# Opening of a two-layer attention kernel: weight sums on VectorE beside the first keys' product, bias columns and means in column tiles, vectors loaded as rows

## The chip, the core and the metric

The kernel runs on one core of a Trainium2 chip. The metric is the device time of one execution in microseconds (us); lower is better. The core has five engines with an instruction stream each: TensorE (PE, matrix products), VectorE (DVE), ScalarE (ACT), GpSimd (POOL) and SyncE (SP, which here only issues transfers). They wait for each other through semaphores. Transfers between the chip's memory (DRAM) and the on-chip memory (SBUF) run on 16 DMA engines. Matrix products are written to a small memory of their own, PSUM, in banks of 128 partitions x 512 float32 values.

## The reference

The input is `x`, 8 images of 512 channels by 32 x 32 points, in float32. Two layers follow each other, here cut to what is computed:

```python
# layer 0, on tokens: S = 1024 tokens of C = 512 channels per image
xn = layer_norm(x_flat, gamma, beta)                      # over channels, eps 1e-5
q = xn @ Wq.T + bq;  k = xn @ Wk.T + bk;  v = xn @ Wv.T + bv    # 8 heads of 64
attn = softmax(q @ k.T / sqrt(64))                        # per head
out = (attn @ v) @ Wo.T + bo + x_flat

# layer 1, on channels: group norm over 32 groups, then one head over all 512 channels
h = group_norm(x, gamma, beta)
q = wq @ h + bq;  k = wk @ h + bk;  v = wv @ h + bv
attn = softmax(q.T @ k * 512 ** -0.5)
out = x + wp @ (attn applied to v) + bp
```

## The kernel before

Almost every large product is done by a scheme of seven half-size products in place of eight (a Strassen-like one): both operands are cut into 2 x 2 blocks, some sums of blocks are formed (`S1` to `S4` of the weights, `T1` to `T4` of the data), and seven steps (`STEPS`) of matmuls follow, with additions on VectorE that put the results together. Weights are used again for each of the 8 images. Their blocks and sums are therefore formed once in the opening, saved to DRAM, and loaded again in each later image.

Two weight products are formed once as well: `a`, from the second layer's query and key weights, and `m`, from its value and output weights, so that the second layer needs fewer projections. With them come three small vectors: `ua` (the query bias carried through the key weights), `bm` and `bo` (value biases carried through the output weights).

Each engine runs the instructions in the order in which this program writes them (`ORDERED`: TensorE, ScalarE, VectorE; GpSimd's order is left to a scheduler). `later` puts a small piece of work into a list, and `tick` takes pieces from it between the steps of a product.

```python
STEPS = [
    ("11", "11", "x", True),
    ("12", "21", "z", True),
    ("S2", "T2", "x", False),
    ("S1", "T1", "y", True),
    ("S3", "T3", "x", False),
    ("22", "T4", "z", True),
    ("S4", "22", "y", False),
]
SLOTS = ["11", "12", "22", "S1", "S2", "S3", "S4"]
    # ... (cut)
    vt = const.tile([P, len(VECS), NC], F32, tag="vecs", name="vecs")
    with nc.allow_non_contiguous_dma(reason="per-channel vectors, once"):
        for i, n in enumerate(VECS):
            nc.scalar.dma_start(out=vt[:, i, :], in_=vecs[n].rearrange("(c p) -> p c", p=P))
    # ... (cut)
    wq, wk = (load_chunks(n) for n in ("q1", "k1"))
    bq1_row = half_tile("bq1_row")
    nc.sync.dma_start(out=bq1_row, in_=vecs["bq1"].rearrange("(a c) -> a c", a=1).to_broadcast((P, C)))
    x_next = load_x(0)
    wv, wp = (load_chunks(n) for n in ("v1", "p1"))
    # ... (cut)
    def sums_of_blocks(engine, w):
        engine.tensor_add(w["S1"], w["21"], w["22"])
        engine.tensor_sub(w["S2"], w["S1"], w["11"])
        engine.tensor_sub(w["S3"], w["11"], w["21"])
        engine.tensor_sub(w["S4"], w["12"], w["S2"])
    # ... (cut)
    def complete(n, w):

        sums_of_blocks(nc.gpsimd, w)
        save_w(n, w)
        return w

    wk_now, wv_now = first_w("k"), first_w("v")
    wo = first_w("o")
    wq_now = first_w("q")
    # ... (cut)
    def product(dst, lhs, rhs, n, g):
        ps = wide_psum(f"psw_{n}_{g}")
        for k in range(2):
            for oc in range(NC):
                nc.tensor.matmul(ps[:, ts(k, C)], lhs[oc][:, ts(2 * g + k, P)], rhs[oc],
                                 start=(oc == 0), stop=(oc == NC - 1))
        for i in range(2):
            nc.scalar.copy(dst[f"{i + 1}{g + 1}"], ps.rearrange("p (a o) -> p a o", a=2)[:, :, ts(i, CB)])

    def columns(dst, lhs, rhs, n, plus):

        ps = bank(f"ps{n}")
        for o in range(NC):
            for c in range(NC):
                nc.tensor.matmul(ps[:, o : o + 1], lhs(c, o), rhs(c), start=(c == 0), stop=(c == NC - 1))
        nc.vector.tensor_add(dst, ps[:, :NC], vt[:, VECS.index(plus), :])
    # ... (cut)
    # class Product: one of the seven steps
        def step(self, n=1):
            for _ in range(n):
                i = self.done
                self.done += 1
                a, b, to, opens = STEPS[i]
                until(lambda: a in self.a and b in self.b)
                if opens and not hasattr(self, to):
                    setattr(self, to, self.banks(to))
                self.part(getattr(self, to), self.a[a], self.b[b], opens)
                tick(self.pieces)
                if i == 0:
                    self.u1 = self.copy((0, 0))
                elif i == 1:
                    self.out(0, 0, self.u1, self.z)
                elif i == 2:
                    self.u2 = self.copy((0, 1))
                elif i == 4:
                    u3 = self.copy((1, 1))
                    self.out(1, 1, u3, self.y)
                    self.u3 = u3
                elif i == 5:
                    if self.shift.twice:
                        self.u3 = self.copy((1, 0))
                    self.out(1, 0, self.u3, self.z)
                elif i == 6:
                    self.out(0, 1, self.u2, self.y)
                if i in (2, 4, 6):
                    self.finish()
    # ... (cut)
    # class LayerNorm (for image b)
        def over_channels(self, ps):
            for k in range(NH):
                nc.tensor.matmul(ps[:, ts(k, HB)], ones_c, self.total[:, ts(k, HB)], start=True, stop=True)
    # ... (cut)
        def mean(self):
            ps = wide_psum(f"mean_{self.b}")
            self.over_channels(ps)
            self.mu = big_tile(f"mu_{self.b}")
            nc.scalar.copy(self.mu, ps)
    # ... (cut)
        def variance(self):

            ps = bank(f"var_{self.b}")
            for k in range(NH):
                nc.tensor.matmul(ps[ts(k, D), :], ones_c[:, :D], self.total[:, ts(k, HB)], start=True, stop=True)
            self.ps = ps
    # ... (cut)
    with tc.manual_schedule(engines=ORDERED):
        nq = natural(wq, "q1")
        nk = natural(wk, "k1")
        ln = LayerNorm(0, x_next)
        pieces = ln.steps()

        def norm(n):
            for _ in range(n):
                next(pieces, None)

        norm(5)
        wa = weight_tiles("a_first")
        product(wa, nq, nk, "a", 0)
        norm(3 + 4 + 3)
        nv = natural(wv, "v1")
        product(wa, nq, nk, "a", 1)
        columns(bm, lambda c, oc: wp[c][:, ts(oc, P)], lambda c: vec("bv1", c), "bm", "bp1")
        norm(100)
        for k in range(NH):
            for j in range(2):
                for a in range(2):
                    ln.affine(j, k, a)
        hb = operands(ln.result())
        add_operands(hb)
        until(lambda: not side)
        complete("k", wk_now)
        complete("v", wv_now)
        complete("o", wo)
        wm = weight_tiles("m_first")
        product(wm, nv, wp, "m", 0)
        columns(bo, lambda c, oc: wo[f"{oc // 2 + 1}{c // 2 + 1}"][:, c % 2, ts(oc % 2, P)],
                lambda c: vec("bv0", c), "bo", "bo0")
        product(wm, nv, wp, "m", 1)
        complete("q", wq_now)
        complete("a", wa)
        complete("m", wm)
        for c in range(NC):
            t = half_tile(f"uat_{c}")
            nc.vector.scalar_tensor_tensor(t, wk[c], 1.0, bq1_row, ALU.mult, ALU.mult, accum_out=ua[:, c : c + 1])
        kt = all_of(project("k0", wk_now, bias_of("bk0"), hb))
```

The sums that `complete` asks for, four for each of six sets of weights, run on GpSimd; `ua` is made by four VectorE instructions that multiply a 128 x 512 half of the key weights with the bias row and add up along the row. `columns` forms a vector by matmuls with one column each. A float32 matmul appears in the profile as two passes, so 16 matmuls are 32 records.

Of the kernel before, what the change touches and what calls it, by code (L numbers as in the profile page):

```python
# [11 lines left out]
F32 = mybir.dt.float32  # L12
# [4 lines left out]
ORDERED = {mybir.EngineType.PE, mybir.EngineType.Activation, mybir.EngineType.DVE}  # L17
# [48 lines left out]
def fast_path(ctx: ExitStack, tc: tile.TileContext, x: bass.AP, vecs: dict, weights: dict, out: bass.AP,  # L66
# [56 lines left out]

    def load_x(b):
# [33 lines left out]
    ident = const.tile([P, P], F32, tag="ident", name="ident")  # L158
    make_identity(nc, ident)
    ones_c = const.tile([P, P], F32, tag="ones_c", name="ones_c")  # L160
    nc.vector.memset(ones_c, 1.0 / C)
    ones = const.tile([P, P], F32, tag="ones", name="ones")
    nc.vector.memset(ones, 1.0)
    grp = const.tile([P, P], F32, tag="grp", name="grp")
    group_matrix(nc, grp)
    eps = const.tile([P, 1], F32, tag="eps", name="eps")
    nc.vector.memset(eps, EPS)
    checks = const.tile([P, B * (HEADS // 2 + 1)], F32, tag="checks", name="checks")
    nc.vector.memset(checks, 0.0)
    n_checks = [0]  # L170
# [70 lines left out]
    def complete(n, w):  # L241

        sums_of_blocks(nc.gpsimd, w)
        save_w(n, w)
        return w
# [3 lines left out]
    wq_now = first_w("q")  # L249

# [1149 lines left out]
```

## Time and profile before

| what | value |
|---|---|
| time, median of 3 runs | 3009.26 us (3009.22 to 3010.62) |
| span of the profiled execution | 3008.7 us |
| TensorE busy | 2965.4 us, 99% |
| VectorE busy | 1787.4 us, 59% |
| ScalarE busy | 1035.2 us, 34% |
| GpSimd busy | 47.9 us, 2% |
| moved by DMA | 217.34 MB, mean 72 GB/s |

The page gives the busy time of each engine, and also the span in 40 equal slices of about 75 us, with the busy share of each slice in tenths (9 is 90% or more). Here the opening is the first slice and part of the second:

```
PE   7999999999999999999999999999999999999898
POOL 5100000000000000000000000000000000000000
DMA  8003141031400313003120123101231021301201
```

GpSimd works in the opening and nearly nowhere else. Busy time of an engine includes the time in which an instruction has begun and is held up, so a busy engine is not always one that advances. The chain of waits is followed back from the last instruction to whatever released it, and lists pieces in order of time: what stands in it is what the end of the span waited for. A group line gives the line of the kernel, the engine, the operation, the tile written and the tiles read, the shape, the count, then busy time and the mean of one instruction in ns, then the idle time of the engine before them and what ended it.

### The profile page before, as it was taken

How to read it: one execution, taken by the hardware profiler on the slowest of the kernel's cores; microseconds unless marked ns; L12 is line 12 of the kernel's file. 1: busy time of each engine (PE TensorE's matmuls, PEld its weight loads, DVE VectorE, ACT ScalarE, POOL GpSimd, SP SyncE). 2: the span in 40 equal slices, each digit the busy share in tenths (PEclk: the TensorE clock that was granted, in tenths of full speed). 3: DMA queues.
4: the chain of work that ended last, by engine and by line, in shares of the span. 5: the costliest groups of instructions: out<-in, count | busy, mean ns of one | idle time of the engine just before them, and what ended most of it. 6: DMA issues, size and time to landing. Idle time of an engine off the chain costs nothing.

```text
span 3008.7 us, 26701 instructions
## 1 busy us (share of the span) xinstructions
PE 2965.4 (99%) x10066; PEld 1385.9 (46%) x10066; DVE 1787.4 (59%) x2241; ACT 1035.2 (34%) x1623; POOL 47.9 (2%) x57
## 2 busy tenths in 40 slices
PE   7999999999999999999999999999999999999898
PEld 4533455334553445434554345533455334553344
DVE  6567546674466744666547665467555675436744
ACT  3263213623146221551215512164222632125220
POOL 5100000000000000000000000000000000000000
PEclk9999999999999999999999999999999999999999
DMA  8003141031400313003120123101231021301201
GB/s 283 36 25 108 49 133 41 12 137 40 135 32 25 133 39 122 25 25 133 58 104 25 57 102 108 53 25 60 98 115 46 25 97 61 98 35 46 84 1 57
DMA packets 91162, 217.34 MB, mean 72 GB/s; under 512 B 14992, under 2 KB 19088, under 8 KB 91024
## 3 DMA queue, kind: packets, MB, share of 16 engines
q1 hardware_dynamic: 81616, 204.51, 19.6%
q0 software_dynamic: 3072, 11.01, 0.9%
q8 instruction: 81, 1.33, 0.2%
q10 hardware_dynamic: 6336, 0.03, 0.1%
q14 instruction: 57, 0.47, 0.1%
HBM read 156.26 MB, written 59.24 MB: 72 GB/s over the span
## 4 chain that ended last, share of the span: by engine, by line
PE 93%; DVE 3%; DMA 2%; issue 1%; ACT 0%; SPq 0%; DVEq 0%; ACTq 0%
PE s L657 15%; PE acc L672 14%; PE x_o L403 5%; PE x_s L395 5%; PE y_s L395 4%; PE y_o L403 4%; PE z_o L403 4%; PE z_s L395 4%; PE x_q L378 3%; PE x_vm L387 3%; PE x_qa L378 3%; PE x_v L387 3%; PE x_k L378 3%; PE y_k L378 2%; PE y_q L378 2%; PE z_qa L378 2%
## 5 line engine op out<-in xcount | busy, mean ns | idle before, releaser
L660 ACT ACTIVATE p<-s 128x1024 f32<-128x1024 f32 x512 | 476.3, 1057 | 85.2 <-PE s L657 85.2
L666 DVE TENSOR_TENSOR sum<-sum,p 128x1024 f32<-128x1024 f32 x384 | 470.5, 1225 | 41.4 <-DVE sum L666 0.9
L672 PE MATMUL acc<-p,v 128*64 128x512 f32 x2048 | 453.6, 595 | 0.0
L657 PE MATMUL s<-q,k_again 64*128 64x512 f32 x1792 | 403.3, 600 | 0.3
L672 PEld LDWEIGHTS acc<-p,v 128*64 128x64 f32 x2048 | 141.3, 137 | 305.1 <-issue 293.0
L657 PEld LDWEIGHTS s<-q,k_again 64*128 64x128 f32 x1792 | 161.8, 186 | 240.5 <-ACT p L660 120.1
L664 DVE TENSOR_TENSOR sum<-p,p 128x1024 f32<-128x1024 f32 x64 | 78.4, 1225 | 201.6 <-ACT p L660 201.6
L395 PE MATMUL x_s<-S_qa,T_gn 128*128 128x512 f32 x256 | 120.3, 592 | 0.0
L403 PE MATMUL x_o<-T_p,S_vm 128*128 128x512 f32 x256 | 115.1, 593 | 0.0
L675 ACT COPY o<-acc 128x512 f32<-128x512 f32 x64 | 37.5, 586 | 217.4 <-PE acc L672 217.0
L757 ACT ACTIVATE p<-p 128x512 f32<-128x512 f32 x128 | 80.7, 630 | 73.1 <-DVE p L317 73.1
L317 DVE TENSOR_TENSOR p<-u(1, 1)_s,y_s 128x512 f32<-128x512 f32 x32 | 22.0, 688 | 132.3 <-ACT u(1, 1)_s L408 132.3
L425 ACT ACTIVATE u(0, 0)_k<-x_k,vecs 128x512 f32<-128x512 f32 x16 | 11.0, 687 | 232.0 <-PE x_k L378 232.0
L694 ACT COPY rr<-r 32x16 f32<-32x16 f32 x256 | 51.6, 202 | 102.5 <-DVE r L631 99.4
L470 DVE STREAM_TRANSPOSE rden<-rr 128x512 f32<-128x512 f32 (+1 forms) x72 | 55.3, 768 | 37.0 <-ACT rr L694 23.4
L403 PEld LDWEIGHTS x_o<-T_p,S_vm 128*128 128x128 f32 x256 | 48.7, 190 | 61.2 <-issue 61.2
L395 PEld LDWEIGHTS x_s<-S_qa,T_gn 128*128 128x128 f32 x256 | 48.7, 190 | 61.2 <-issue 60.9
L317 DVE TENSOR_TENSOR y<-u(1, 1)_o,y_o 128x512 f32<-128x512 f32 x16 | 11.0, 688 | 109.1 <-ACT u(1, 1)_o L408 109.1
L378 PE MATMUL x_out<-T_o,w_o 128*128 128x512 f32 x128 | 61.5, 604 | 3.2 <-DVE T_o L457 3.2
L387 PE MATMUL x_vm<-w_m,T_gn 128*128 128x256 f32 x256 | 60.5, 379 | 0.0
L395 PE MATMUL y_s<-S_qa,gn 128*128 128x512 f32 x128 | 60.2, 593 | 0.0
L395 PE MATMUL x_s<-qa,gn 128*128 128x512 f32 x128 | 60.2, 592 | 0.0
(330 smaller groups left out, 4441.8 us busy)
## 6 DMA issues: line engine op xcount, KB each, us to landing
x<-in_x_dram SPq DMA_DIRECT2D x32, 512.0 KB, 7.8
xr<-in_x_dram SPq DMA_DIRECT2D x64, 256.0 KB, 4.2
x_away<-x SPq DMA_DIRECT2D x32, 512.0 KB, 2.8
x1r<-x_away SPq DMA_DIRECT2D x64, 256.0 KB, 3.3
out_dram<-y SPq DMA_DIRECT2D x64, 256.0 KB, 2.1
k_away<-k SPq DMA_DIRECT2D x28, 512.0 KB, 2.6
k_again<-k_away SPq DMA_DIRECT2D x28, 512.0 KB, 4.5
w_o<-saved_o SPq DMA_DIRECT2D x24, 512.0 KB, 5.4
```

What stands on the lines that cost most here:

```text
L378: nc.tensor.matmul(dst, a[:, k, ts(r, P)], b[:, k, :], start=(opens and k == 0), stop=(k == 1), skip_group_check=True)
L387: nc.tensor.matmul(dst[:, ts(m, CB)], b[:, k, ts(2 * r + m, P)], a[:, k, :], start=(opens and m == 0 and k == 0), stop=(k == 1), skip_grou ...
L395: nc.tensor.matmul(dst, b[:, k, ts(r, P)], a[:, k, :], start=(opens and k == 0), stop=(k == 1), skip_group_check=True)
L403: nc.tensor.matmul(dst, a[:, m, ts(r, P)], b[m // 2][:, m % 2, :], start=(opens and m == 0), stop=(m == NM // 2 - 1), skip_group_check=True)
L470: nc.vector.transpose(t.rearrange("p (k i) -> p k i", i=BL), r.unsqueeze(2).to_broadcast((P, r.shape[1], BL)))
L657: nc.tensor.matmul(s[:, ts(i, HB)], self.k[m // 4][r, ts(m % 4, P)], self.q[r, :], start=True, stop=True)
L660: nc.scalar.activation(p, s, AF.Exp, scale=1.0 / float(D) ** 0.5)
L664: nc.vector.tensor_add(self.sum, self.p[0], p)
L666: nc.vector.tensor_add(self.sum, self.sum, p)
L672: nc.tensor.matmul(acc[i * D : (i + 1) * D, :], value_of(self.vt, m, self.c * P + i * D, D), self.p[m][:, ts(i, HB)], start=(m == 0), stop ...
L694: nc.scalar.copy(rr[n][ts(j, BL), :], r[ts(2 * n + j // 2, BL), :])
L757: nc.scalar.activation(dest(i, k), dest(i, k), AF.Exp, scale=float(C) ** -0.5)
```

## The change

The change is to the opening, and to the mean of each layer norm.

- The sums `S1` to `S4` of the first layer's key weights stay on GpSimd, and are asked for at the very start. Those of the five other sets (`v`, `q`, `o`, `a`, `m`), and the four instructions for `ua`, become pieces for VectorE, two of which are taken between any two steps of the first keys' product. GpSimd's order is now fixed by the program too, and it issues the saves. This is for keeping GpSimd's arithmetic from running beside VectorE's, and for letting the keys' product begin before the sums are all there.
- `bm` and `bo` are made differently: the bias vector is set into the first column of four 32-column tiles of zeros, each of which takes one 128-row part of the weights and writes to 32 partitions of its own in one bank; a ones column then adds up the four rows. This replaces many matmuls of one column by a few long ones in column tiles.
- The mean of a layer norm is written as two tiles of 64 columns, one for each half of the tokens, into one bank, as the variance was before. Four copies on ScalarE then spread it to all partitions, where one copy did before.
- The twelve vectors are loaded as 48 rows of 128 contiguous values, and turned into columns by one transpose on TensorE, instead of being scattered by the transfer value by value. The broadcast bias row for `ua` is loaded after the weights instead of before `x`.

The diff, without its parts that only move lines:

```diff
@@ -14,7 +14,8 @@
-ORDERED = {mybir.EngineType.PE, mybir.EngineType.Activation, mybir.EngineType.DVE}
+POOL = mybir.EngineType.Pool
+ORDERED = {mybir.EngineType.PE, mybir.EngineType.Activation, mybir.EngineType.DVE, POOL}
@@ constants (moved here from below the loads, cut) @@
+    with tc.manual_schedule(engines={POOL}):
... (cut: the same constants)
+    vrows = const.tile([len(VECS) * NC, P], F32, tag="vrows", name="vrows")
+    for i, n in enumerate(VECS):
+        nc.scalar.dma_start(out=vrows[ts(i, NC), :], in_=vecs[n].rearrange("(c p) -> c p", p=P))
+    vt = const.tile([P, len(VECS), NC], F32, tag="vecs", name="vecs")
@@ -129,11 +150,6 @@
-    vt = const.tile([P, len(VECS), NC], F32, tag="vecs", name="vecs")
-    with nc.allow_non_contiguous_dma(reason="per-channel vectors, once"):
-        for i, n in enumerate(VECS):
-            nc.scalar.dma_start(out=vt[:, i, :], in_=vecs[n].rearrange("(c p) -> p c", p=P))
-
     def vec(n, c):
         i = VECS.index(n)
         return vt[:, i, c : c + 1]
@@ loads (constants moved up, cut) @@
     wq, wk = (load_chunks(n) for n in ("q1", "k1"))
-    bq1_row = half_tile("bq1_row")
-    nc.sync.dma_start(out=bq1_row, in_=vecs["bq1"].rearrange("(a c) -> a c", a=1).to_broadcast((P, C)))
     x_next = load_x(0)
     wv, wp = (load_chunks(n) for n in ("v1", "p1"))
... (cut: constants moved up)
+    bq1_row = half_tile("bq1_row")
@@ -209,14 +209,16 @@
             d, t = saved_part(n, w, g)
             nc.gpsimd.dma_start(out=d, in_=t)
 
-    def sums_of_blocks(engine, w):
-        engine.tensor_add(w["S1"], w["21"], w["22"])
-        engine.tensor_sub(w["S2"], w["S1"], w["11"])
-        engine.tensor_sub(w["S3"], w["11"], w["21"])
-        engine.tensor_sub(w["S4"], w["12"], w["S2"])
-
     SUMS = {"S1": ("add", "21", "22"), "S2": ("subtract", "S1", "11"), "S3": ("subtract", "11", "21"),
             "S4": ("subtract", "12", "S2")}
+
+    def sum_of_blocks(engine, w, n):
+        op, l, r = SUMS[n]
+        engine.tensor_tensor(w[n], w[l], w[r], getattr(ALU, op))
+
+    def sums_of_blocks(engine, w):
+        for n in SLOTS[3:]:
+            sum_of_blocks(engine, w, n)
 
     def sum_later(w, n, new, view):
 
@@ -242,11 +244,17 @@
 
         sums_of_blocks(nc.gpsimd, w)
         save_w(n, w)
-        return w
+
+    def complete_later(n, w):
+
+        for name in SLOTS[3:]:
+            later(lambda name=name: sum_of_blocks(nc.vector, w, name))
+        later(lambda: save_w(n, w))
 
     wk_now, wv_now = first_w("k"), first_w("v")
     wo = first_w("o")
     wq_now = first_w("q")
+    nc.sync.dma_start(out=bq1_row, in_=vecs["bq1"].rearrange("(a c) -> a c", a=1).to_broadcast((P, C)))
 
     def natural(t, n):
 
@@ -271,13 +279,29 @@
         for i in range(2):
             nc.scalar.copy(dst[f"{i + 1}{g + 1}"], ps.rearrange("p (a o) -> p a o", a=2)[:, :, ts(i, CB)])
 
-    def columns(dst, lhs, rhs, n, plus):
-
-        ps = bank(f"ps{n}")
-        for o in range(NC):
+    class Columns:
+
+
+
+        def __init__(self, dst, v, plus):
+            self.dst, self.v, self.plus = dst, VECS.index(v), VECS.index(plus)
+            self.z = half_tile(f"z_{v}").rearrange("p (c i) -> p c i", i=BL)[:, :NC, :]
+            nc.vector.memset(self.z, 0.0)
+            nc.vector.tensor_copy(self.z[:, :, 0], vt[:, self.v, :])
+
+        def rows(self, w):
+            ps = bank("ps_rows")
             for c in range(NC):
-                nc.tensor.matmul(ps[:, o : o + 1], lhs(c, o), rhs(c), start=(c == 0), stop=(c == NC - 1))
-        nc.vector.tensor_add(dst, ps[:, :NC], vt[:, VECS.index(plus), :])
+                for cols, part in w(c):
+                    nc.tensor.matmul(ps[ts(c, BL), cols], self.z[:, c, :], part, start=True, stop=True)
+            self.r = half_tile("rows")
+            nc.scalar.copy(self.r, ps)
+
+        def columns(self):
+            ps = bank("ps_columns")
+            for o in range(NC):
+                nc.tensor.matmul(ps[:, o : o + 1], self.r[:, ts(o, P)], ones[:, :1], start=True, stop=True)
+            nc.vector.tensor_add(self.dst, ps[:, :NC], vt[:, self.plus, :])
 
 
 
@@ -488,8 +512,9 @@
             self.b, self.xt = b, xt
 
         def over_channels(self, ps):
+
             for k in range(NH):
-                nc.tensor.matmul(ps[:, ts(k, HB)], ones_c, self.total[:, ts(k, HB)], start=True, stop=True)
+                nc.tensor.matmul(ps[ts(k, D), :], ones_c[:, :D], self.total[:, ts(k, HB)], start=True, stop=True)
 
         def add(self, name, k, l, r):
 
@@ -502,10 +527,12 @@
             yield
 
         def mean(self):
-            ps = wide_psum(f"mean_{self.b}")
+            ps = bank(f"mean_{self.b}")
             self.over_channels(ps)
             self.mu = big_tile(f"mu_{self.b}")
-            nc.scalar.copy(self.mu, ps)
+            for k in range(NH):
+                for r in range(2):
+                    nc.scalar.copy(self.mu[ts(r, D), ts(k, HB)], ps[ts(k, D), :])
 
         def rows(self, t, k):
             return t[:, ts(k, HB)].unsqueeze(1).to_broadcast((P, 2, HB))
@@ -518,11 +545,8 @@
             nc.scalar.activation(wide(self.sq[j, k]), wide(self.xt[j, k]), AF.Square)
 
         def variance(self):
-
-            ps = bank(f"var_{self.b}")
-            for k in range(NH):
-                nc.tensor.matmul(ps[ts(k, D), :], ones_c[:, :D], self.total[:, ts(k, HB)], start=True, stop=True)
-            self.ps = ps
+            self.ps = bank(f"var_{self.b}")
+            self.over_channels(self.ps)
 
         def root(self):
             self.var = compact(half_tile(f"vart_{self.b}"), self.ps)
@@ -873,13 +892,19 @@
             for _ in range(n):
                 next(pieces, None)
 
+        complete("k", wk_now)
         norm(5)
         wa = weight_tiles("a_first")
         product(wa, nq, nk, "a", 0)
+        ps = bank("ps_vecs")
+        nc.tensor.transpose(ps[:, : len(VECS) * NC], vrows, ident[: len(VECS) * NC, : len(VECS) * NC])
+        nc.vector.tensor_copy(vt.rearrange("p v c -> p (v c)"), ps[:, : len(VECS) * NC])
+        bm_columns, bo_columns = Columns(bm, "bv1", "bp1"), Columns(bo, "bv0", "bo0")
         norm(3 + 4 + 3)
         nv = natural(wv, "v1")
+        bm_columns.rows(lambda c: [(slice(0, C), wp[c])])
         product(wa, nq, nk, "a", 1)
-        columns(bm, lambda c, oc: wp[c][:, ts(oc, P)], lambda c: vec("bv1", c), "bm", "bp1")
+        bm_columns.columns()
         norm(100)
         for k in range(NH):
             for j in range(2):
@@ -888,21 +913,24 @@
         hb = operands(ln.result())
         add_operands(hb)
         until(lambda: not side)
-        complete("k", wk_now)
-        complete("v", wv_now)
-        complete("o", wo)
         wm = weight_tiles("m_first")
         product(wm, nv, wp, "m", 0)
-        columns(bo, lambda c, oc: wo[f"{oc // 2 + 1}{c // 2 + 1}"][:, c % 2, ts(oc % 2, P)],
-                lambda c: vec("bv0", c), "bo", "bo0")
+        bo_columns.rows(lambda c: [(ts(i, CB), wo[f"{i + 1}{c // 2 + 1}"][:, c % 2, :]) for i in range(2)])
         product(wm, nv, wp, "m", 1)
-        complete("q", wq_now)
-        complete("a", wa)
-        complete("m", wm)
-        for c in range(NC):
+        bo_columns.columns()
+
+        def score_bias(c):
             t = half_tile(f"uat_{c}")
             nc.vector.scalar_tensor_tensor(t, wk[c], 1.0, bq1_row, ALU.mult, ALU.mult, accum_out=ua[:, c : c + 1])
-        kt = all_of(project("k0", wk_now, bias_of("bk0"), hb))
+
+        for n, w in (("v", wv_now), ("q", wq_now), ("o", wo), ("a", wa), ("m", wm)):
+            complete_later(n, w)
+        later(*(lambda c=c: score_bias(c) for c in range(NC)))
+        units, kt = project("k0", wk_now, bias_of("bk0"), hb)
+        for u in units:
+            u.pieces = 2
+            u.rest()
+        until(lambda: not side)
 
         def next_values_and_queries(b, wv, wq):
```

More of the change, by code (lines that the diff above doesn't have):

```diff
@@ L121, in fast_path @@
         name=nc.get_next_instruction_name(), act_func_set_id=list(tables).index("natural_log_exp_and_others")))
+    with tc.manual_schedule(engines={POOL}):
+        ident = const.tile([P, P], F32, tag="ident", name="ident")
+        make_identity(nc, ident)
+        ones_c = const.tile([P, P], F32, tag="ones_c", name="ones_c")
+        nc.vector.memset(ones_c, 1.0 / C)
+        ones = const.tile([P, P], F32, tag="ones", name="ones")
+        nc.vector.memset(ones, 1.0)
+        grp = const.tile([P, P], F32, tag="grp", name="grp")
+        group_matrix(nc, grp)
+        eps = const.tile([P, 1], F32, tag="eps", name="eps")
+        nc.vector.memset(eps, EPS)
+        checks = const.tile([P, B * (HEADS // 2 + 1)], F32, tag="checks", name="checks")
+        nc.vector.memset(checks, 0.0)
+        n_checks = [0]
+    vrows = const.tile([len(VECS) * NC, P], F32, tag="vrows", name="vrows")
+    for i, n in enumerate(VECS):
+        nc.scalar.dma_start(out=vrows[ts(i, NC), :], in_=vecs[n].rearrange("(c p) -> c p", p=P))
+    vt = const.tile([P, len(VECS), NC], F32, tag="vecs", name="vecs")
     def load_x(b):
@@ L151, in fast_path @@
     wq, wk = (load_chunks(n) for n in ("q1", "k1"))
-    bq1_row = half_tile("bq1_row")
-    nc.sync.dma_start(out=bq1_row, in_=vecs["bq1"].rearrange("(a c) -> a c", a=1).to_broadcast((P, C)))
     x_next = load_x(0)
     wv, wp = (load_chunks(n) for n in ("v1", "p1"))
[L158 to L170, printed above, removed]
+    bq1_row = half_tile("bq1_row")
     ua = const.tile([P, NC], F32, tag="ua", name="ua")
@@ L859, in bias_of @@
         return lambda oc: vec(n, oc)
-    def all_of(units):
-        for u in units[0]:
-            u.rest()
-        return units[1]
     with tc.manual_schedule(engines=ORDERED):
```

## The prediction

> **What bounds the kernel now.** I read the busy shares first, then the chain of waits for the first 200 us, then the timeline of that stretch engine by engine, because the page says TensorE is 99% busy over the span (2965.4 of 3008.7 us) and only the first of its 40 slices is below 9 tenths by much. TensorE is the bound; what can be won is either TensorE work or TensorE idleness, and the idleness lies in the opening. The chain there (start us, us, what):
>
> ```profile
> 57.11 4.41 DVE T_h L457
> 61.52 0.39 issue
> 61.92 0.15 DVE bo L280
> 62.06 18.47 DVE uat L904 x8
> 80.53 0.61 DVE k L317
> 81.14 0.04 issue
> 81.19 3.78 PE z_k L378 x4
> 84.97 2.73 PE y_k L378 x4
> 87.70 1.72 PE x_k L378 x4
> ```
>
> TensorE stands behind four VectorE products (`uat`, L904) for 14.6 us: they sit in VectorE's order ahead of the first addition that frees a bank of the keys' product. Then the same four matmul passes that take 1.72 us at full clock take 3.78 and 2.73: 3.1 us more. The stretches of 10 us show it (columns after the stretch: TensorE, weight loads, VectorE, ScalarE, GpSimd busy with instruction counts, clock, DMA share, GB/s):
>
> ```profile
> 60.00:70.00 10.00, 6.61 (x16) 2.66 (x14) 10.00 (x5) 2.42 (x4) 9.97 (x11) 0.99 0.40 157
> 70.00:80.00 10.00, 0.00 (x0) 0.00 (x0) 10.00 (x5) 0.00 (x0) 9.97 (x12) 0.50 0.41 158
> 80.00:90.00 10.00, 8.81 (x14) 3.86 (x15) 3.11 (x6) 0.55 (x1) 3.34 (x5) 0.66 0.48 185
> ```
>
> VectorE is "busy" with five instructions in 10 us, and GpSimd is full. The groups of the first 100 us say why:
>
> ```profile
> L904 DVE SCALAR_TENSOR_TENSOR uat<-w_k,bq_row 128x512 f32<-128x512 f32 x4 | 18.5, 4685 | 0.0
> L501 DVE TENSOR_TENSOR lns<-lns 128x512 f32<-128x512 f32 x2 | 1.4, 691 | 0.1
> L545 DVE TENSOR_TENSOR x<-x,rstd 128x1024 f32<-128x1024 f32 x4 | 7.3, 1880 | 0.0
> L514 DVE TENSOR_TENSOR x<-x,mu 128x1024 f32<-128x1024 f32 x4 | 4.6, 1221 | 2.3 <-ACT mu L508 2.3
> L524 PE MATMUL var<-lnq,ones_c 128*64 128x512 f32 x4 | 2.9, 1086 | 0.0
> ```
>
> A 128x512 operation on two SBUF operands costs 0.69 us when GpSimd rests (L501) and 4.69 us beside its sums. In the timeline each `uat` ends while GpSimd issues transfers between two groups of sums. The scaling of L545 (1.88 against 1.22 for the same shape in L514) and the four `T_h` (11.5 us together from 50.48 to 62.0, against 4 x 1.22 = 4.9) are stretched likewise.
>
> [...] 4.69 against 0.69 us, while the `k` additions at 80.46 and 81.06, one operand in PSUM, take 0.68 us beside a running GpSimd sum. [...] the eight passes of a `den` (four 32-column tiles) stand 1.0 us apart from what follows, the four passes of a later `var` (two 64-column tiles) take 1.01 us, and the four of a `mean` over all 128 columns 1.72 us. [...] The trace agrees at 70 to 80 us (0.50 after 14.6 us idle), and shows also 0.50 in 36 to 38 us, just after the 32 one-column `psbm` passes (the four `var` passes take 2.9 us there)[...]. [...] In the trace the vectors' queue moves 0.03 MB in 6336 packets, for 3.5% of the first 100 us, so 3.5 us of every DMA engine.
>
> **The change part by part.**
>
> 1. *Sums leave GpSimd.* Of six sets of four, one (`k`) stays there, and runs when its blocks land; 20 sums go to VectorE between the keys' steps, two pieces a step. Cost on VectorE: 20 x 0.69 = 13.8, the four `uat` now uncontended at about 0.77 (0.69 + 0.08 for the accumulator read, an estimate) = 3.1, the eight additions 8 x 0.69 = 5.5: 22.4 us. The keys' product is 14 steps x 1.72 = 24.1 us on TensorE. VectorE fits, with little room. Laying its order against the steps, the additions that TensorE waits for still end about when they are needed, and VectorE finishes its last pieces some 2 us after TensorE; the value product that follows loads VectorE to half (4.0 and 5.2 of 10 us at 100 to 120), so this is absorbed. Before, the stage took from 57.87 (first `x_k`) to 99.60 (first `x_v`): 41.7 us. After: 24.1 plus about 0.7 of small waits, 24.8. Gain 17 us, of which 14.6 is the stall and 3.1 the clock.
>
> 2. *The start of the keys' product.* First load side: the vector packets (3.5 us per DMA engine) and the 0.26 MB bias row ahead of `x` go away. The second half of `w_k` waits for the second half of `w_q` to land, in both kernels; with clear queues I put `w_q` whole at about 5.5, `w_k` at 8.5, ScalarE free of issues at about 7.5, its copies of about 1 us after that, and the first `psw_a` at 11 instead of 14.36. Then TensorE's own work to `x_k`: `psw_a` 7.1, transposed vectors 0.3, `mean` 1.0, `pst_v` 1.9, bias rows 1.1 (column tiles, as `den`), `psw_a` 7.1, columns (8 one-column passes x 0.11) 0.9, `var` 1.2, `psw_m` 7.1, rows 1.1, `psw_m` 7.1, columns 0.9: 36.8 us, so 48 if nothing is waited for. Before, these places held 2 x 3.6 us of one-column passes, and the slow clock after each (`var` 2.9 instead of 1.0; the second `psw_m` 8.8 instead of 7.1).
>    But `var` waits for VectorE: mean at 19, its copies from ScalarE now in four of 0.59 (two are enough to start), centring from 20.2: 4.9, squares' sums 3.8; and GpSimd's four `k` sums (4 x 1.3 = 5) now fall just there, as the blocks land at about 22. 20.2 + 8.7 + 5 = 33.9, where TensorE could begin `var` at 30 (11 + 7.1 + 0.3 + 1.0 + 1.9 + 1.1 + 7.1 + 0.9): a wait of 3.5 us, perhaps with a slow clock after it. From there TensorE needs 17.4 to `x_k` (51.3), VectorE 0.7 + 4.0 + 4.9 + 4.9 + small = 15 to the last `T_h` (49), now without GpSimd. So `x_k` at about 52 with a share for the clock, against 57.87. Gain 6 us.
>
> 3. *Means in column tiles, seven more times.* Passes 1.72 become 1.01, and the next group takes 1.91 instead of 1.72, as behind `var`: 0.52 each, 7 x 0.52 = 3.6 us. It is TensorE work in a row without gaps, so it counts. The copies grow on ScalarE from 1.01 to 4 x 0.59 = 2.3 us, in a stretch where it is a quarter busy; the next `u` copy then ends about 3.0 us after the mean, while TensorE needs it at 3.4.
>
> Sum: 17 + 6 + 3.6 = 26.6 us; 3009.3 - 26.6 = 2982.7. I say 2982.5.
>
> **The rivals.** (a) VectorE becomes the bound of the keys' stage: 22.4 us of 24.1, with two-SBUF operations everywhere. Against: no GpSimd arithmetic is left then, only issuing; at 75 to 80 us a `uat` ended during such issuing, so issuing doesn't hold VectorE off. If it did, or if the `uat` form costs more than 0.77, the stage takes 28 to 30: about 2987. (b) The 14.6 us stall was hidden anyway by a later wait. Against: from 99.6 on the chain is TensorE step after step, without a wait up to 200 us; nothing there gives time back. If half were lost, 2990. (c) The early `k` sums hold VectorE off more than once over, as they did `uat`, and the late saves (9 MB, five sets, now packed into some 25 us, near the 390 to 410 GB/s seen at 20 to 40 us) delay the tiles that wait for their buffers: the value product's third result waits for a save. I put that save's landing at 25 us after the product begins, and the need at some 33. If late by 5 us: 2988. (d) The loads gain more, the collision misses `var`, and `x_k` starts at 48: 2978.
>
> **Range and chances.** The 14.6 us stall is nearly sure to go, and the means' 3.6 are copied from a measured neighbour; 20 us are solid. The spread comes from the opening's start (plus or minus 4) and the tightness of VectorE (up to 5). 8 in 10: 2976 to 2990. Two per cent are 60 us, and the whole stage that is touched is 100 us of which TensorE needs over 60; faster by over 2% has 0.01. Slower by over 2% needs a new stall in every batch, and the order of instructions after the opening is the same but for the means: 0.01.
>
> **What would show it.** Right: no TensorE idleness above 2 us between the first `x_k` and `x_v`, 25 us apart; `uat` below 1 us; sums near 0.69; clock at full through 50 to 80 us; `mean` four passes in 1.0 us in every batch; first `psw_a` near 11. Wrong: sums well above 0.69 us beside GpSimd's issues; the `k` additions as what TensorE waits for; `var` later than 36; a wait for a save at the third value result; or waits on `mu` that TensorE feels in later batches.

## The result and the profile after

| | before | after |
|---|---|---|
| time, median of 4 runs, measured together | 3009.94 us (3009.22 to 3011.54) | 2983.94 us (2980.97 to 2986.1) |
| span of the profiled execution | 3008.7 us | 2983.8 us |
| TensorE busy | 2965.4 us | 2956.7 us |
| first `x_k` (start of the first keys' product) | 57.87 us | 53.43 us |
| first `x_v` (its end) | 99.60 us | 77.71 us |

The ratio is 0.9912 (95%: 0.9895 to 0.9929), 26 us less. The two last rows are starts in the timeline; the chain puts the same starts up to 0.2 us later.

The chain of waits of the changed kernel, in order of time (start us, us, what), from layer norm's sums of squares to the next layer norm's mean:

```profile
27.09 2.23 DVE lnq L522
...
29.34 1.65 DVE lnq L526
30.99 2.20 DVE lnq L522
33.19 0.07 DVE bm L304
33.27 1.61 DVE lnq L526
...
34.91 1.94 PE var L517 x2
36.85 7.84 PE psw_m L277 x16
44.70 1.02 PE ps_rows L296 x16
45.72 7.06 PE psw_m L277 x16
52.78 0.79 PE ps_columns L303 x8
53.57 1.83 PE x_k L402 x4
55.40 1.72 PE z_k L402 x4
...
76.11 1.77 PE y_k L402 x4
77.87 1.73 PE x_v L411 x8
...
93.41 1.01 PE mean L517 x4
94.42 1.92 PE x_v L411 x8
```

Where `uat` stood for 18.47 us and `z_k` then took 3.78, there are now 14 steps of 1.72 to 1.83 us in a row. What VectorE holds up in the opening now is the variance: four `lnq` operations end one behind the other before the second half of `var`. The bias rows and columns are 1.02 and 0.79 us long. The stretches of 10 us show the same stage (columns as in the table of before):

```profile
50.00:60.00 10.00, 10.00 (x31) 4.93 (x30) 6.87 (x12) 2.45 (x4) 2.66 (x5) 1.00 0.40 159
60.00:70.00 10.00, 10.00 (x25) 4.31 (x24) 7.35 (x13) 1.95 (x3) 4.60 (x9) 1.00 0.91 351
70.00:80.00 10.00, 10.00 (x30) 5.30 (x29) 7.46 (x17) 2.32 (x4) 2.85 (x6) 1.00 0.94 357
```

TensorE is full and at clock 1.00, and VectorE does 12 to 17 instructions in 10 us where it did five. GpSimd's busy time is the issue of saves only. The VectorE groups of the first 80 us (shape and count, then busy us and mean ns of one, then idle before):

```profile
L522 DVE TENSOR_TENSOR lnq<-sq,sq 128x1024 f32<-128x1024 f32 x2 | 4.6, 2290 | 0.0
L526 DVE TENSOR_TENSOR lnq<-lnq 128x512 f32<-128x512 f32 x2 | 3.3, 1642 | 0.0
L217 DVE TENSOR_TENSOR w_a_first<-w_a_first,w_a_first 128x512 f32<-128x512 f32 x4 | 2.7, 688 | 0.0
L924 DVE SCALAR_TENSOR_TENSOR uat<-w_k,bq_row 128x512 f32<-128x512 f32 x4 | 2.7, 686 | 0.0
L481 DVE TENSOR_TENSOR T_h<-x,T_h 128x1024 f32<-128x1024 f32 x2 | 2.4, 1224 | 0.2 <-ACT x L573 0.2
```

`uat` fell from 4685 to 686 ns and `T_h` is at 1224 ns, while `lnq` is at 2290 ns in the shape in which `T_h` takes 1224: it runs beside the only sums left on GpSimd. In the waits of TensorE (us in total, times, longest) the 14.6 us of `z_k` are gone and one for `var` is new; the one for `T_o`, in the last image, is as before:

```profile
PE x_out L402 <- DVE T_o L481: 3.2, 1, 3.2
PE var L517 <- DVE lnq L526: 1.5, 1, 1.5
```

### The profile page after: what moved, and what is told of

It reads as the page before. It is cut to its first block, busy times and chain, and to the rows that moved or that the text cites. A ratio compares the mean times of both kernels' runs of the same rounds, so it can differ in the third digit from the quotient of the medians.

```text
span 2983.8 us, 26676 instructions
## 1 busy us (share of the span) xinstructions
PE 2956.7 (99%) x10043; PEld 1374.4 (46%) x10043; DVE 1777.3 (60%) x2266; ACT 1047.1 (35%) x1649; POOL 22.0 (1%) x37
## 4 chain that ended last, share of the span: by engine, by line
PE 97%; DVE 2%; DMA 1%; issue 0%; ACT 0%; SPq 0%; DVEq 0%
PE s L681 15%; PE acc L696 15%; PE x_o L427 6%; PE x_s L419 6%; PE y_s L419 4%; PE y_o L427 4%; PE z_s L419 4%; PE z_o L427 4%; PE x_q L402 3%; PE x_k L402 3%; PE x_qa L402 3%; PE x_vm L411 3%; PE x_v L411 3%; PE x_out L402 2%; PE y_k L402 2%; PE y_q L402 2%
```

## The experiments

Two questions were open. Which of the four parts makes which share? And is it the move of the sums to VectorE that removes the stall, or only the new place of the four `uat`, which now stand behind additions for which they used to hold TensorE? Ten other kernels answer, and the changed kernel was timed once more beside two of them. All keep the whole computation. First the table, with starts from the timeline of each (us), stage = first `x_v` less first `x_k`, and the median time against the kernel before in the same comparison:

| kernel | first x_k | first x_v | stage | time | before | ratio (95%) |
|---|---|---|---|---|---|---|
| before | 57.87 | 99.60 | 41.7 | | | |
| changed | 53.43 | 77.71 | 24.3 | 2983.94 | 3009.94 | 0.9912 (0.9895 to 0.9929) |
| only the sums | 61.07 | 85.27 | 24.2 | 2995.64 | 3012.22 | 0.9945 (0.9928 to 0.9962) |
| only `uat` behind | 59.60 | 83.80 | 24.2 | 2994.58 | 3012.22 | 0.9941 (0.9924 to 0.9957) |
| only the means | 59.62 | 101.36 | 41.7 | 3007.93 | 3012.22 | 0.9987 (0.9980 to 0.9994) |
| only the columns | 52.96 | 94.64 | 41.7 | 3005.32 | 3012.22 | 0.9976 (0.9968 to 0.9985) |
| only the vectors | 56.16 | 96.14 | 40.0 | 3008.92 | 3012.18 | 0.9989 (0.9981 to 0.9998) |
| changed, no columns | 56.74 | 80.93 | 24.2 | 2986.20 | 3012.18 | 0.9914 (0.9898 to 0.9931) |
| changed, no rows | 56.17 | 80.45 | 24.3 | 2986.52 | 3012.18 | 0.9915 (0.9896 to 0.9934) |
| changed, GpSimd sums | 49.95 | 74.23 | 24.3 | 2979.50 | 3012.18 | 0.9890 (0.9874 to 0.9907) |
| changed, again | 52.89 | 77.17 | 24.3 | 2983.01 | 3011.90 | 0.9901 (0.9884 to 0.9917) |
| changed, `k` sums on VectorE | 50.18 | 74.40 | 24.2 | 2979.66 | 3011.90 | 0.9892 (0.9875 to 0.9908) |
| changed, `uat` ahead, GpSimd sums | 48.95 | 91.06 | 42.1 | 2994.47 | 3011.90 | 0.9942 (0.9925 to 0.9958) |

One kernel's times spread by 1.7 us (four runs) to 10.9 us (twenty), so where two kernels differ by 3 us the trace carries the reading and the time only agrees. Starts in a trace spread too: two profiles of the changed kernel differ by 0.5 us at the first `x_k`, and the kernel with only `uat` behind, whose instructions up to there are those of the kernel before, begins the product 1.7 us later, because the end of `x` landed later (VectorE's sum of it begins at 22.10 us instead of 20.50). Durations within a chain are the safer reading.

### Only the sums

The kernel before with the sums and `uat` as pieces between the keys' steps, GpSimd's order fixed, and the early `k` sums:

```diff
+        complete("k", wk_now)
         norm(5)
...
-        complete("k", wk_now)
-        complete("v", wv_now)
-        complete("o", wo)
...
-        complete("q", wq_now); complete("a", wa); complete("m", wm)
-        for c in range(NC): ...  # the four uat
-        kt = all_of(project("k0", wk_now, bias_of("bk0"), hb))
+        for n, w in (("v", wv_now), ("q", wq_now), ("o", wo), ("a", wa), ("m", wm)):
+            complete_later(n, w)
+        later(*(lambda c=c: score_bias(c) for c in range(NC)))
+        units, kt = project("k0", wk_now, bias_of("bk0"), hb)
+        for u in units: u.pieces = 2; u.rest()
```

> The kernel before with the first part of the change alone: key sums early on GpSimd, the other 20 sums and the four uat as VectorE pieces beside the keys' product; vectors, bias columns and means as before. My theory [...]: the keys' stage, first x_k to first x_v, falls from 41.7 to about 25 us; uat below 1 us; first x_k stays within 2 us of 57.9, since TensorE is dense up to it; time about 3009.9 - 16 = 2994. Rival (the stage is short in the changed kernel only because the other parts bring x and the weights earlier): the stage stays above 30 us, time above 3000.

Measured: 16.6 us less. The stage is 24.2 us, 17.5 shorter, so the rival, that the other parts make it short, is refuted. The product begins 3.2 us later than before, not within 2 us as expected. Of this, 1.7 us is the spread just named; against the kernel with only `uat` behind, where `x` landed as late, the rest is `psbm` at 4.43 us instead of 3.47 and the first `psw_m` at 8.01 instead of 7.50.

### Only `uat` behind the keys' product

Two statements of the kernel before change places; every sum stays on GpSimd:

```diff
         complete("m", wm)
+        kt = all_of(project("k0", wk_now, bias_of("bk0"), hb))
         for c in range(NC):
             t = half_tile(f"uat_{c}")
             nc.vector.scalar_tensor_tensor(t, wk[c], 1.0, bq1_row, ALU.mult, ALU.mult, accum_out=ua[:, c : c + 1])
-        kt = all_of(project("k0", wk_now, bias_of("bk0"), hb))
```

> The kernel before with one thing moved: the four uat stand behind the eight additions of the keys' product in VectorE's order; all sums stay on GpSimd. Theory A (it is the order: slow two-SBUF operations stand ahead of additions that don't collide): no stall although GpSimd sums go on beside the product, stage about 25 us, additions 0.69 us, T_h still stretched, time about 2993. Theory B (the sums have to leave GpSimd for the stage to run): additions stretched as uat was, or uat again holding up the value product, stage or what follows it still over 35 us, time above 3002.

Measured: 17.6 us less, as much as the sums' move brings. The timeline (start us, us, engine, line, operation, count, and in brackets the idle time before and its end) shows why the sums may stay:

```profile
74.97 1.27 POOL L216 TENSOR_TENSOR w_a_first<-w_a_first,w_a_first 128x512 f32<-128x512 f32 x1
...
75.44 0.69 DVE L317 TENSOR_TENSOR k<-u(0, 0)_k,z_k 128x512 f32<-128x512 f32 x1 [2.82 <-PE z_k L378]
...
84.61 0.68 DVE L905 SCALAR_TENSOR_TENSOR uat<-w_k,bq_row 128x512 f32<-128x512 f32 x1
```

The addition `k`, which frees the bank TensorE waits for, reads one operand from PSUM and takes 0.69 us in the midst of a GpSimd sum. All eight additions of the product took 0.69 us, and GpSimd's last sum ended at 82.82 us, before `uat` begins at 84.61. So the whole stall came through four VectorE instructions in front of a fifth that GpSimd did not hold up.

### Only the means

`over_channels` and `mean` as in the change, in all eight layer norms, nothing else.

> The kernel before with only the means in two 64-column tiles and four copies. My theory: 0.6 to 0.7 us of TensorE work less in each of seven later images, the first one hidden in the opening, nothing else moves: about 3009.9 - 4.5 = 3005.4. Rival (the longer copies on ScalarE delay a copy that TensorE waits for): period from mean to mean not below 363.9 us, time 3009 or more.

Measured: 4.3 us less by 20 runs, as expected (the 95% interval of the ratio means 1.8 to 6.0 us). The start of the first product says nothing here: its own profiled execution was a long one for this kernel (span 3010.7 us).

### Only the columns

`Columns` in place of `columns`, in the kernel before:

```diff
-    def columns(dst, lhs, rhs, n, plus):
...
-                nc.tensor.matmul(ps[:, o : o + 1], lhs(c, o), rhs(c), start=(c == 0), stop=(c == NC - 1))
+    class Columns:
...
+                    nc.tensor.matmul(ps[ts(c, BL), cols], self.z[:, c, :], part, start=True, stop=True)
```

> The kernel before with only the bias columns made through rows in 32-column tiles. TensorE saves 2 x 2 us and the slow clock behind each group (1.9 and 1.7 us), so x_k may start 4 to 7 us earlier. Theory A (that start is hidden behind the uat stall, whose end is set by VectorE and GpSimd): stall longer by as much, time within 2 us of before. Theory B (it counts by itself): 3003 to 3005.

Measured: 6.9 us less (3005.32). The theory that the stall would swallow this gain fell. The chain:

```profile
34.45 0.79 PE ps_columns L295 x8
35.24 1.94 PE var L540 x4
...
47.94 2.79 DVE T_h L473
50.83 5.87 DVE T_h L473 x3
...
57.43 18.50 DVE uat L922 x8
76.58 3.78 PE z_k L394 x4
...
94.80 1.73 PE x_v L403 x8
```

The stall is untouched (`uat` 18.50 us, stage 41.7), but it begins 4.6 us sooner, at 57.43 instead of 62.06. The bias passes stood ahead of `var`, and behind `var` come the scaling and the `T_h`, and behind these `uat`. A stall swallows a gain only if its end is set from elsewhere; this one is a piece of VectorE work, 18.5 us long, whose start hung on the same TensorE work. But that path carries only 1.0 of the 4.6 us. VectorE's timeline has the scaling and the last `T_h`, first in the kernel before, then here:

```profile
43.28 7.28 DVE L545 TENSOR_TENSOR x<-x,rstd 128x1024 f32<-128x1024 f32 x4
57.11 4.88 DVE L457 TENSOR_TENSOR T_h<-x,T_h 128x1024 f32<-128x1024 f32 x1
...
42.30 5.71 DVE L561 TENSOR_TENSOR x<-x,rstd 128x1024 f32<-128x1024 f32 x4
55.07 2.29 DVE L473 TENSOR_TENSOR T_h<-x,T_h 128x1024 f32<-128x1024 f32 x1
```

The scaling begins 1.0 us sooner; it then takes 1.6 us less and the last `T_h` 2.6 less beside GpSimd's sums, the first three `T_h` 0.5 more. So most of the gain is two-input VectorE work that met GpSimd's sums at other moments. No run shows whether that would hold with other loads.

### Only the vectors

Rows and one transposition, and the bias row for `uat` after the weights:

```diff
-            nc.scalar.dma_start(out=vt[:, i, :], in_=vecs[n].rearrange("(c p) -> p c", p=P))
+    for i, n in enumerate(VECS):
+        nc.scalar.dma_start(out=vrows[ts(i, NC), :], in_=vecs[n].rearrange("(c p) -> c p", p=P))
...
+        nc.tensor.transpose(ps[:, : len(VECS) * NC], vrows, ident[: len(VECS) * NC, : len(VECS) * NC])
```

> The kernel before with only the vectors loaded as rows (one transpose to columns) and the bias row loaded after the weights. Before on the chip of the earlier runs was 3012.2. Theory A (loads land earlier, so the layer norm and with it the uat stall start and end earlier): first psw_a near 12.2 us instead of 14.4, x at 18 instead of 20.5 or later, stall unchanged in length, time 2 to 3 us below before. Theory B (hidden, as the stall's end hangs on GpSimd's sums): within 1 us of before.

Measured: 3.3 us less (3008.92; the 95% interval of the ratio means 0.6 to 5.7 us), first `x_v` 3.5 us sooner. The first `psw_a` begins at 12.20 instead of 14.36 us, and the first `x_k` 1.7 us sooner; the rest is in the stage, where TensorE waits 13.3 us instead of 14.6.

### The changed kernel with the old columns

> The changed kernel with the bias columns made as before by one-column matmuls. Bias columns alone gave 6.9 us in the kernel before. Theory A (they lie on TensorE's and the layer norm's path here too): x_k 5 to 7 us later than 53.6, slow clock again behind both groups, time 5 to 7 us above the changed kernel's 2984. Theory B (here the wait for var covers the first group): 3 to 4 us above.

The edit takes `Columns` out of the changed kernel and puts `columns` back. Measured: 2986.20 us, 2.3 and 3.2 us above the two medians of the changed kernel, and in the trace 3.2 us later at the first `x_v`; the theory of 5 to 7 us was wrong, the rival's 3 to 4 about right. The chain shows what the columns removed:

```profile
29.51 4.58 PE psbm L287 x32
34.09 2.82 PE var L501 x4
36.92 7.85 PE psw_m L277 x16
44.76 3.47 PE psbo L287 x32
48.23 8.67 PE psw_m L277 x16
```

`psbm` here lies within the time in which the changed kernel waits for `lnq`, so removing it saved nothing: `var` ends at 36.91 us here and at 36.85 there, and the `psw_m` behind it takes 7.85 and 7.84. The second vector counts whole: `psbo` and the `psw_m` after it, 3.47 + 8.67 = 12.1, against 1.02 + 7.06 + 0.79 = 8.9 in the changed kernel, 3.3 us.

### The changed kernel with the vectors loaded value by value

> The changed kernel with the vectors loaded value by value as before (12 transfers of 512 elements; the bias row stays late). Theory A (the start of the loads is on the path): psw_a at 14 instead of 12.2, x_k 1.5 to 3 us later, time 2 to 3 us above 2984. Theory B (VectorE's chain to var hides it): within 1 us.

Twelve loads of single values as before, no transposition; the bias row stays late. Measured: 2986.52 us; first `psw_a` at 15.26 instead of 12.22, the second pair of `var` at 39.30 instead of 34.91, first `x_v` 2.7 us later. Undone the part costs about what it brings alone, 3.5 us, within the spread of the starts.

### The changed kernel with the sums back on GpSimd

The sums are asked for where the kernel before asks for them, GpSimd's order is left to the scheduler, and the four `uat` stand behind the keys' product:

```diff
-        complete("k", wk_now)
         norm(5)
...
         until(lambda: not side)
+        complete("k", wk_now)
+        complete("v", wv_now)
+        complete("o", wo)
...
-        for n, w in (("v", wv_now), ("q", wq_now), ("o", wo), ("a", wa), ("m", wm)):
-            complete_later(n, w)
-        later(*(lambda c=c: score_bias(c) for c in range(NC)))
+        complete("q", wq_now); complete("a", wa); complete("m", wm)
         units, kt = project("k0", wk_now, bias_of("bk0"), hb)
         for u in units:
-            u.pieces = 2
             u.rest()
+        for c in range(NC): score_bias(c)
```

> The changed kernel with all 24 sums on GpSimd where the kernel before has them (its order left to the scheduler again) and the four uat behind the keys' product; means, bias columns and rows stay. uat_behind showed that the additions of the keys' product are not held up by GpSimd. Theory A (the sums' move to VectorE is worth nothing beyond the order of uat): stage 24 to 25 us, and as the early key sums no longer stand in front of var, x_k at 51 to 54: time 2981 to 2986, equal to the changed kernel. Theory B (sums beside the layer norm and T_h hold TensorE up at the third step, which needs T_h): a wait of 2 us or more in the stage, time 2987 or more.

Measured: 2979.50 us, below the 2981 to 2986 of theory A, and the first `x_v` 3.5 us sooner than in the changed kernel. Theory B's wait is not there. The stretches, with GpSimd full all through the keys' product:

```profile
50.00:60.00 10.00, 10.00 (x25) 4.41 (x25) 5.01 (x5) 2.97 (x5) 9.97 (x11) 1.00 0.51 200
60.00:70.00 10.00, 10.00 (x25) 4.39 (x24) 2.29 (x4) 1.46 (x3) 9.97 (x11) 1.00 0.45 172
```

TensorE is as full as in the changed kernel. VectorE's eight additions are untouched; two of the four `uat`, which begin at 75.04, are stretched to 2.27 and 1.88 us, and nobody waits for them. The stage is equal to a tenth; the 3.5 us are won ahead of it.

### The changed kernel with its `k` sums on VectorE

This asks where those 3.5 us come from. The `k` sums go from GpSimd, where they ran at 26.6 to 34.3 us beside `lnq`, to VectorE behind the `T_h`:

```diff
-        complete("k", wk_now)
         norm(5)
...
         until(lambda: not side)
+        sums_of_blocks(nc.vector, wk_now)
+        save_w("k", wk_now)
```

> The changed kernel with one thing moved: the four sums of the key weights from GpSimd, where they run beside the layer norm's squares, to VectorE behind the four T_h. Theory A (they are what delays var, and x_k with it): lnq additions 1.22 and 0.69 us again, var about 3 us earlier, no slow clock behind it, first x_k at 50 to 51, time 3 to 3.5 us below the changed kernel. Theory B (the four sums, 2.8 us more on VectorE in front of the keys' third step, hold TensorE up instead): a wait of 1 us or more at the third step, gain under 1.5 us.

Measured: 2979.66 us, against 2983.01 of the changed kernel in the same comparison; first `x_v` 2.8 us sooner. VectorE's timeline:

```profile
27.04 1.22 DVE L522 TENSOR_TENSOR lnq<-sq,sq 128x1024 f32<-128x1024 f32 x1
28.29 0.69 DVE L526 TENSOR_TENSOR lnq<-lnq 128x512 f32<-128x512 f32 x1
```

and the chain of the same kernel:

```profile
32.46 1.93 PE var L517 x4
34.39 7.06 PE psw_m L277 x16
```

`lnq` is back at 1.22 and 0.69 us (2.30 and 1.65 in the changed kernel), `var` ends at 34.39 instead of 36.85, and the `psw_m` behind it takes 7.06 instead of 7.84. These 2.46 and 0.78 make up the 3.2 us by which the first `x_k` comes sooner than in the first profile of the changed kernel (50.18 and 53.43); 0.5 of it is the spread between its two profiles (53.43 and 52.89).

### The changed kernel with GpSimd sums and `uat` ahead

Against the kernel with the sums on GpSimd, only four VectorE instructions change places:

```diff
         complete("m", wm)
+        for c in range(NC): score_bias(c)
         units, kt = project("k0", wk_now, bias_of("bk0"), hb)
         for u in units:
             u.rest()
-        for c in range(NC): score_bias(c)
```

> The changed kernel without its first part: all 24 sums on GpSimd and the four uat ahead of the keys' product, as in the kernel before; means, bias columns and rows as changed. It differs from the run with the sums back on GpSimd (2979.5) only in the place of four VectorE instructions. Theory (their place makes the whole stall): uat at 4.7 us each, TensorE idle for 13 to 15 us, slow clock after it, first x_k near 50 as there, first x_v at 90 to 93 instead of 74.4, time 2995 to 2998. Rival (with earlier loads GpSimd is done sooner and the stall shrinks): below 2990.

Measured: 2994.47 us, 15 us more than with `uat` behind. The wait is back whole:

```profile
PE z_k L395 <- DVE k L334: 14.7, 1, 14.7
```

### The changed kernel again

> The changed kernel itself, unchanged, beside the next two on one chip, as their measure: 2981 to 2987, first x_k at 53 to 54 us, first x_v at 77 to 79.

Measured: 2983.01 us, within the earlier runs; first `x_k` at 52.89 instead of 53.43.

## Why the prediction was right, and where not

Predicted 2982.5, measured 2983.94: right. At the first `x_v` 23 us were to be gained and 21.9 are there; 3.6 more were to follow and 3.0 did. Behind these sums one step holds for half of its reason only, and some terms were mis-sized. That the total came so close is in part luck: the start of the product fell 1.6 us short, and the last image lost 1.9 us that nothing in the working provides for, while the periods between the means gave more than the means themselves.

1. *Sums leave GpSimd*, stage 24.8 us, gain 17. Measured 24.3 and 17.4, with full clock (1.00 from 50 to 80 us) and no wait. The sums cost 0.69 us beside GpSimd's issues, `uat` 0.69 + 0.085 for the accumulator, as the working had it, and the rival of VectorE as the bound did not come. But the cause that the step names, sums on GpSimd, is only half of it. By these runs it took both: VectorE instructions on two SBUF operands beside GpSimd's sums (`uat` at 4.69 us, without them at 0.69), and their place ahead of the first `k` addition. Taking the place alone removes the stall (`uat` behind: stage 24.2), and with the place put back it is there again (`uat` ahead: 14.7). The prediction had the evidence, since it says that the `k` additions take 0.68 us beside a running sum, and did not draw the conclusion. That the sums make `uat` slow rests on its 0.69 us wherever GpSimd does no sums; a kernel with the sums moved and `uat` still ahead was not run, and at 0.69 + 0.085 us each these four would still hold TensorE for up to 3 us (an estimate). The move of the sums to VectorE is worth nothing: 2995.64 us with it and 2994.58 with `uat` behind alone, 2979.66 and 2979.50 with the other parts. With the `k` sums' early start it costs 3 us.

2. *The start of the keys' product*, `x_k` at about 52, gain 6. Measured 53.4 and 4.4 (52.9 and 5.0 in the second profile). The mis-sized terms: the first `psw_a` at 12.2 instead of 11, as `w_k` was whole at 9.96 us and not at 8.5; `mean` 1.69 in place of 1.0; and `var`, put at 1.2, takes 1.93 even at full clock and without a wait (the kernel with the `k` sums on VectorE, at clock 1.00 from 30 to 40 us), since the last `lnq` stands behind the addition for `bm` in VectorE's order and is not there when `var` begins. So of the 2.9 us that `var` took before, 0.9 was slow clock (0.50 from 36 to 38 us) and not 1.9. The collision of the `k` sums with layer norm was foreseen and came: 5 us of delay predicted, 7.68 us of sums measured, `lnq` 7.7 us in all in place of 3.8, and `var` late. Its price was given as a wait of 3.5 us "perhaps with a slow clock"; it was a wait of 1.5, about 0.9 of slow `var` and 0.8 in `psw_m` (clock 0.75 from 34 to 36 us, 0.50 to 38, 0.90 to 40), 3.2 together, and the experiment without the collision gave back as much. What the step did not weigh is that this price belongs to the change: the kernel before ran three of its four `k` sums later, from 50.36 us on.

3. *Means*, 0.52 us each, 3.6. Measured alone 4.3 us. In TensorE's work the term is right: a mean takes 1.01 instead of 1.72 us and the group behind it 1.92 instead of 1.73, so 0.52 together. In the traces the six full periods from the mean of the second image to that of the last take 2183.75 us before and 2179.66 after, 0.68 each; 0.12 of this is that TensorE's waits for `x` at `y_out` fell from 1.3 to 0.6 us in all. With the means alone the periods take 2182.37 us, 0.23 less each, with 2.8 us of these waits. Such small waits differ from kernel to kernel by as much as the means bring, and what sets them was not tried.

The parts done alone give 16.6 + 6.9 + 3.3 + 4.3 = 31.1 us, the whole 26.0 in one comparison and 28.9 in another. The columns explain part of the difference: 6.9 alone but 3.2 when undone in the changed kernel. There the first group is hidden by the wait for `lnq`, and no stretched scaling or `T_h` is left to shorten. What remains is not resolved by these runs.

At the last mean the traces are 25.9 us apart, ahead of the wait for `T_o` in the last image 26.8, and at the end 24.9. The 1.9 us are lost in the last image: both kernels wait 3.2 us for `T_o`, and the first four passes behind it took 3.26 us before and 3.78 after, the next group 2.35 and 3.18 (1.3 us), at a clock of 0.59 and 0.56 in the two stretches from 2824 to 2828 us before and of 0.50 from 2797 to 2802 after; another 0.6 goes in the group norm and the product `qa` behind it (0.50 from 2850 to 2854 us before, from 2822 to 2830 after). What sets how much slow clock follows such a wait was not tried.

## What to carry to other kernels

When an engine is slowed by another one's work, ask first who waits for the slowed instructions: moving four of them behind the addition that frees a bank won as much as moving 20 sums to another engine (17.6 and 16.6 us). A gain ahead of a stall isn't lost if the stall's start hangs on the same work, as the columns show (6.9 us); but look where it comes from, since most of theirs was contention that fell elsewhere (1.6 us in the scaling, 2.6 in the last `T_h`). And work that is brought forward to relieve a later stage lands beside something: the early `k` sums doubled layer norm's sums (2.29 and 1.64 us instead of 1.22 and 0.69), and leaving all the sums on GpSimd, or these four on VectorE behind `T_h`, gives the two best kernels here, 2979.5 and 2979.66 us.

## What the runs showed of the hardware

- Behind long groups of one-column matmuls the next passes were nearly always slow, with TensorE busy throughout. In the changed kernel with the old columns, the four passes of `var` behind the 32 one-column passes of `psbm` take 2.82 us instead of 1.93, and `psw_m` behind `psbo` takes 8.67 instead of 7.06. The stretches of this kernel (columns as above) show the granted clock:

```profile
32.00:34.00 2.00, 2.00 (x10) 2.00 (x10) 0.72 (x1) 0.00 (x0) 2.00 (x2) 0.50 1.11 350
34.00:36.00 2.00, 2.00 (x5) 0.58 (x5) 0.76 (x2) 0.00 (x0) 2.00 (x4) 0.50 0.97 334
36.00:38.00 2.00, 2.00 (x4) 0.64 (x3) 0.72 (x1) 0.29 (x1) 0.62 (x2) 0.50 0.97 364
```

  Six of the kernels have two such groups each. In the timelines `var` takes 2.89 us behind five of the first groups, and `psw_m` 8.81 to 10.02 behind all six second ones; the kernel with the `k` sums on VectorE, at clock 1.00 from 30 to 40 us, has 2.00 and 7.13. The clock itself is shown for three of these eleven: above, and in the kernel before, 0.50 from 36 to 38 us and from 50 to 52. The exception is the first group of the kernel with only the vectors, behind which `var` and `psw_m` take no longer than at clock 1.00:

```profile
29.89 3.63 PE L279 MATMUL psbm<-vecs,w_p 128*128 128x1 f32 x32
33.45 2.00 PE L524 MATMUL var<-lnq,ones_c 128*64 128x512 f32 x4
35.38 7.13 PE L269 MATMUL psw_m<-w_p,nat_v 128*128 128x512 f32 x16
```

  What decides was not tried.

- In the changed kernel a wait of 1.5 us, behind the eight one-column passes of `bm` and two passes of `var`, was followed by slow passes (the other two of `var` 1.94 us instead of 1.07, `psw_m` 7.84 instead of 7.06; clock 0.75 from 34 to 36 us and 0.50 from 36 to 38). Without the wait, behind the same passes, `psw_m` took 7.06 (the kernel with the `k` sums on VectorE, clock 1.00 from 30 to 40 us). A wait of 1.69 us just ahead of these one-column passes (the changed kernel with the vectors loaded value by value) was followed by no slow passes: `var` 1.07 us a pair, `psw_m` 7.06. So in these runs the length of the wait alone does not decide.
- The price of contention isn't fixed. Beside GpSimd's sums, `lnq` (128x1024) and most `T_h` took 2.1 to 2.8 us instead of 1.22, one `T_h` of the kernel before 4.88, and `uat` 4.69 instead of 0.69 in one place and 1.88 to 2.27 in another. Its own 0.69 us and one whole sum of 1.28 make 1.97, and 4.69 is more than that. What decides between twice and seven times was not tried.
